# Last stage: shorter turns for eight MLPs, their first squares in the stage in front, earlier experts, a quarter of relu on VectorE

## Chip, cores and metric

The kernel runs on one core of one Trainium2 chip. The metric is the device time of one execution in microseconds (us), as the median of several runs. A profiled execution, recorded by the hardware profiler, gives the span and everything that is said below of single instructions.

## The reference, cut to what matters

The input x has 16 sequences of 256 tokens with 128 features, 4096 tokens in all. Eight sublayers follow each other, each as `x = x + layernorm(f(layernorm(x)))`. The change lies in the seventh sublayer's last part and the eighth sublayer:

```python
# end of L3_attn_ref: attention, then a squared-relu MLP
xa = xa + attn_scale * (y @ o_w)
xa = xa + a_mlp_scale * (square(relu(rms_norm(xa) @ a_fc_w)) @ a_proj_w)   # 128 -> 512 -> 128
# L3_ffn_ref: 8 experts; each expert takes the 64 best of a sequence's 256 tokens
probs = softmax(x @ gate_w)                    # per token over 8 experts
g, m = top_k(probs per expert, 64)
h = gelu(x[m] @ w1[e]) @ w2[e]                 # 128 -> 512 -> 128
out = zeros; out[m] += g * h                   # rounded to bf16
```

Around both stands the outer norm: `x = x + layernorm(xa)`, then `layernorm(x)` is what the experts read, then `x = x + layernorm(out)` is the result.

## The kernel before

All data stay on the chip. The tokens lie in eight groups g = 0 to 7 of 512 tokens (two sequences), each a tile of 128 partitions x 4 x 128 (`xm[g]`, `x[g]`). Work that belongs together is a Python generator; each `yield` ends a step. `Ctx.turns` writes the instruction order by hand: time is counted in turns, an item starts at a given turn, and in each turn every started item gives one step (up to three if it is behind), in the order of the list. Instructions go to their engine's queue in just this order, and each queue is worked through in order. So the start turns and the places of the `yield`s decide what stands in front of what on each engine.

`stage_last` has three kinds of items. `last(g)` is the MLP of one group and what follows it: squares (L1727, GpSimd), their sum (L1730, VectorE), `rsqrt` (L244 and L245, GpSimd), the scaled n (L1735, VectorE), four transposes on TensorE and the copy nT (L1739, ScalarE), four products with `afc` into PSUM (128x512 each, called afc below), each followed by Relu (L1745) and Square (L1746) on ScalarE, sixteen products with `aproj` (called aproj below), the copy ln_y (L1751, ScalarE), the sum with xm (L1753, VectorE), layer norm statistics (L255 and L257 on VectorE, L244 and L245 on GpSimd), the norm (L264, VectorE), the sum into x (L1757, GpSimd), statistics of x, nb = -mean x rs (L1716 and L1717, GpSimd), the normed `exn` on ScalarE (L1720), its transposes and copy xT (L1764), the gate product (128x8), its copy p (L1772), and the softmax into `probs` (L1775 to L1783). `selection(q)` takes the probabilities of two groups, transposes them (L1791), and picks 64 of 256 tokens in eight rounds on VectorE (L1797 and L1799), then the rank of each chosen token by three small products and `slot` (L1818). `pair_of(q, pair)` does two experts for four sequences: one-hot matrices `hot` (L1828, VectorE) and `back` (L1832, GpSimd), the gather as a product into `ps_xin`, transposes of `back` (L1850), products with w1, gelu (L1866), products with w2, and the weighted scatter as a product into `ps_sum`.

Before, `last(g)` starts in the turns 0, 1, 3, 5, 7, 9, 19 and 21, `selection(q)` in 19, 25, 33 and 42, and the first pair of experts in turn 25, the others two turns apart. Groups 6 and 7 thus stand partly among the experts. PSUM has five banks that rotate for nearly all of this (`ps_s`), one for `ps_xin` and two for `ps_sum`.

The stage in front, `l3_gqa` over `attention_stage`, is the attention of the same groups. Its `tail(g)` ends with the sum of the attention output into xm (L1644, GpSimd). In that stage the ScalarE alternates between Exp and Sqrt, and each change is a table load (L1585 for Sqrt, L491 for Exp). Between the two stages the work pool changes, so the first tiles of the last stage wait for the end of what read the old ones, the sum L1644 of group 7 among it.

Of the kernel before, what the change touches and what calls it, by code (L numbers as in the profile page):

```python
# [24 lines left out]
AF = mybir.ActivationFunctionType  # L25
ALU = mybir.AluOpType
AX = mybir.AxisListType
PSUM = bass.MemoryType.PSUM

NB, SEQ, P, D = 16, 256, 128, 128  # L30
NG, NT, GT = 8, 4, 512
# [10 lines left out]
RMS_EPS = float(np.finfo(np.float32).eps)  # L42
# [143 lines left out]
def idle(n):  # L186

    for _ in range(n):
        yield


def bc(ap, axis, n):

    ap = ap.unsqueeze(axis)
    shape = list(ap.shape)
    shape[axis] = n
    return ap.to_broadcast(shape)
# [1408 lines left out]
def l3_gqa(k, xa, w, gain, first):  # L1606

    nc, v = k.nc, k.nc.vector  # L1610

    def head(g, got):
        if g == 0:
            yield
            rot, vs = first
        else:
            rot, vs = yield from l3_rotated(k, xa[g], w)
        yield
        ps = k.transposed_ps(rot, slice(P, 2 * P))
        got["kT"] = k.t([P, GT], "kT", 3)  # L1620
        nc.scalar.copy(got["kT"], ps)
        yield
        got["qT"] = k.t([P, GT], "qT", 2)
        v.tensor_scalar(got["qT"], k.transposed_ps(rot, slice(0, P)), gain, 1.0 / math.sqrt(8.0), ALU.mult, ALU.mult)
        yield
        got["km"] = k.variants(got["kT"], "km")
        yield from idle(6)

        for t in range(NT):
            src = vs[:, t, :].rearrange("p (r d) -> p r d", r=4)  # L1630
            to = k.vm[g % 2][:, t].rearrange("p v (r n) -> p v r n", r=4)
            for u in range(2):
                nc.scalar.copy(to[:, u::2, :, 16 * u : 16 * u + 8], bc(src, 1, 2))
        yield from idle(2)
        got["qm"] = k.variants(got["qT"], "qm")
        yield

    def tail(g, yT):
        yield
        ps = k.tokens_ps(yT, w["o"])  # L1640
        y = k.t([P, NT, D], "y", 2)
        nc.scalar.copy(y, ps)
        yield
        nc.gpsimd.tensor_tensor(xa[g], xa[g], y, ALU.add)  # L1644
        yield

    k.attention_stage(head, 26, 1, tail)


# [52 lines left out]
def stage_last(k, x, xm, w, xn, probs, out):  # L1702
# [4 lines left out]
    nc, v = k.nc, k.nc.vector  # L1707
    ident, ones = k.c["ident"], k.c["ones"]
    ne, cap, nb = 8, 64, 4
    iota = k.c["iota"].rearrange("p (e c) -> p e c", e=2)  # L1710
    slots, sums = {}, {}

    def normed(out, src, mv, rs):

        nb = k.t([P, NT], "ln_nb", 3)
        nc.gpsimd.tensor_scalar(nb, mv[:, :, 0], -1.0, None, ALU.mult)  # L1716
        nc.gpsimd.tensor_tensor(nb, nb, rs, ALU.mult)  # L1717
        yield from idle(2)
        for t in range(NT):
            nc.scalar.activation(  # L1720
                out[:, t, :], src[:, t, :], AF.Identity, bias=nb[:, t : t + 1], scale=rs[:, t : t + 1]
            )

    def last(g):
        xg = xm[g]
        sq = k.t([P, NT, D], "rms_sq", 2)
        nc.gpsimd.tensor_tensor(sq, xg, xg, ALU.mult)  # L1727
        yield
        ss = k.t([P, NT], "rms_ss", 3)
        v.tensor_reduce(ss, sq, AX.X, ALU.add)  # L1730
        rs = k.t([P, NT], "rms_rs", 3)
        k.rsqrt(rs, ss, 1.0 / D, RMS_EPS)
        yield from idle(2)
        n = k.t([P, NT, D], "n", 2)
        v.tensor_tensor(n, xg, bc(rs, 2, D), ALU.mult)  # L1735
        yield
        ps = k.transposed_ps(n)
        nT = k.t([P, GT], "nT", 2)
        nc.scalar.copy(nT, ps)  # L1739
        yield  # L1740
        h = k.t([P, 4, GT], "mlp_h", 4)
        for i in range(4):
            ps = k.ps("s")
            k.mm(ps, w["afc"][:, i * P : (i + 1) * P], nT)
            nc.scalar.activation(h[:, i, :], ps, AF.Relu)  # L1745
            nc.scalar.activation(h[:, i, :], h[:, i, :], AF.Square)  # L1746
            if i % 2:
                yield
        ps = k.tokens_ps(h, w["aproj"].rearrange("p (c n) -> p c n", c=4))
        y = k.t([P, NT, D], "ln_y", 3)  # L1750
        nc.scalar.copy(y, ps)  # L1751
        yield
        v.tensor_tensor(y, y, xg, ALU.add)  # L1753
        mv, rs = k.stats(y)
        yield from idle(2)
        k.normed(y, y, mv, rs)
        nc.gpsimd.tensor_tensor(x[g], x[g], y, ALU.add)  # L1757
        yield
        mv, rs = k.stats(x[g])
        yield from normed(xn[g], x[g], mv, rs)  # L1760
        yield
        ps = k.transposed_ps(xn[g])
        xT = k.t([P, GT], "xT", 2)
        nc.scalar.copy(xT, ps)  # L1764
        yield


        ps = k.ps("s")
        for t in range(NT):
            k.mm(ps[:, t * ne : (t + 1) * ne], xT[:, t * P : (t + 1) * P], w["gate"])  # L1770
        p = k.t([P, NT, ne], "p", 3)
        nc.scalar.copy(p, ps[:, : NT * ne].rearrange("p (t e) -> p t e", t=NT))  # L1772
        yield
        m = k.t([P, NT], "pm", 3)
        v.tensor_reduce(m, p, AX.X, ALU.max)  # L1775
        v.tensor_tensor(p, p, bc(m, 2, ne), ALU.subtract)
        nc.scalar.activation(p, p, AF.Exp)
        yield
        v.tensor_reduce(m, p, AX.X, ALU.add)
        v.reciprocal(m, m)  # L1780
        for b in range(2):
            at, ts = (2 * g + b) * ne, slice(2 * b, 2 * b + 2)
            v.tensor_tensor(probs[:, :, at : at + ne], p[:, ts, :], bc(m[:, ts], 2, ne), ALU.mult)  # L1783
        yield

    def selection(q):

        rows = nb * ne
        ps = k.ps("s")
        for t in range(2):  # L1790
            nc.tensor.transpose(ps[:rows, t * P : (t + 1) * P], probs[:, t, rows * q : rows * (q + 1)], ident)  # L1791
        cur = k.t([rows, SEQ], "top", 2)
        nc.scalar.copy(cur, ps[:rows, :SEQ])
        yield
        for n in range(cap // 8):
            best = k.t([rows, 8], "best", 2)
            v.max(out=best, in_=cur)  # L1797
            nxt = k.t([rows, SEQ], "top", 2)
            v.match_replace(out=nxt, in_to_replace=best, in_values=cur, imm_value=-1.0)  # L1799
            cur = nxt  # L1800
            if n in (2, 5):
                yield
        chosen = k.t([rows, SEQ], "chosen", 1)
        v.tensor_scalar(chosen, cur, 0.0, None, ALU.is_lt)
        yield
        ps = k.ps("s")
        for t in range(2):
            nc.tensor.transpose(ps[:, t * rows : (t + 1) * rows], chosen[:, t * P : (t + 1) * P], ident[:rows, :rows])
        mk = k.t([P, 2, rows], "mk", 2)
        nc.scalar.copy(mk, ps[:, : 2 * rows].rearrange("p (t r) -> p t r", t=2))  # L1810
        yield

        rank = k.ps("s")[:, : 2 * rows].rearrange("p (t r) -> p t r", t=2)
        k.mm(rank[:, 0, :], k.c["before"], mk[:, 0, :])
        k.mm(rank[:, 1, :], ones, mk[:, 0, :], True, False)
        k.mm(rank[:, 1, :], k.c["before"], mk[:, 1, :], False, True)
        slot = slots[q] = k.t([P, 2, rows], "slot", 3)
        v.scalar_tensor_tensor(slot, rank, 1.0, mk, ALU.add, ALU.mult)  # L1818
        v.tensor_scalar(slot, slot, -1.0, None, ALU.add)
        yield  # L1820
# [82 lines left out]

    items = []
    for q in range(4):
        items += [(25 + 8 * q + 2 * pair, pair_of(q, pair)) for pair in range(4)]
    items = items[::-1] + [((19, 25, 33, 42)[q], selection(q)) for q in range(4)]
    items += [((0, 1, 3, 5, 7, 9, 19, 21)[g], last(g)) for g in range(NG)]
    with k.tc.manual_schedule():
        k.turns(items)  # L1910

# [2 lines left out]
def program(ctx: ExitStack, tc: tile.TileContext, xin, dram, at, out):  # L1914
# [92 lines left out]
    with pool("first", "left") as pf:  # L2007
        first = []
        stage("l3m", "left", stage_trunk, l2, rows1["l2b2"], l3, rows3, lm, xm, first, pf, banks=MAMBA_BANKS)
        closed("lm")  # L2010
        with phase("l3g", RING_BANKS):
            l3_gqa(k, xm, l3, l3["gain"], first)
# [4 lines left out]
    en = [pd.tile([P, NT, D], F32, tag=f"exn{g}", name=f"exn{g}") for g in range(NG)]  # L2017
    probs = pd.tile([P, 2, NB * 8], F32, tag="probs", name="probs")
    stage("last", "left", stage_last, xm, last, en, probs, out, banks=LAST_BANKS)
    closed("wd")  # L2020
    closed("we")
# [24 lines left out]
```

## Time and profile before

| what | value |
|---|---|
| median of 3 runs | 2974.41 us (2969.55 to 2975.85) |
| profiled execution | 2974.3 us, its span 2972.5 us |
| mean granted TensorE clock | 0.964 |
| TensorE matmul busy | 2756.0 us, 93% of the span |
| VectorE, ScalarE, GpSimd busy | 1930.3, 1675.4, 1020.9 us |
| last stage | from 2662 us to the end at 2972.5 us |
| TensorE busy from 2660 to 2970 us | 280 of 310 us |

Start times below are us from the start of the span. In the tables by stretch of time the columns are length, then busy time (and instructions) of TensorE matmuls, weight loads, VectorE, ScalarE and GpSimd, then the granted TensorE clock (1.00 is full speed), the DMA share and GB/s. In the chain of waits each row is start, length, engine, tile and line. In a timeline a row is start, length, engine, line, operation, out<-in and count, with the idle time in front and what ended it in brackets. TensorE's fp32 products are recorded as two passes each, so four afc are eight records.

### The profile page before, as it was taken

Reading aid. Unit: us, or ns where it says so; the run is one execution under the profiler, and the core shown is the slowest. Engines: PE = TensorE matmul, PEld = TensorE weight load, DVE = VectorE, ACT = ScalarE, POOL = GpSimd, SP = SyncE. Lnnn points to the kernel's source line nnn. Section 1 sums busy time; section 2 is a strip of 40 time slices with the busy share of each in tenths; the row PEclk is TensorE's granted clock in tenths of the full one; section 3 lists DMA queues with packets and bytes.
Section 4 is the critical chain, followed back from the end, with each engine's and each line's share of the span. In section 5 each row is a group of like instructions: output and inputs, shape, how many; then the busy total and the mean of one; then the engine's idle time right before and its main releaser. Section 6 shows DMA issues by size and latency. Waiting matters only on the chain.

```text
span 2972.5 us, 59427 instructions
## 1 busy us (share of the span) xinstructions
PE 2756.0 (93%) x23673; PEld 1878.9 (63%) x23674; DVE 1930.3 (65%) x5300; ACT 1675.4 (56%) x3528; POOL 1020.9 (34%) x1407
## 2 busy tenths in 40 slices
PE   8889999999998799999978997899999699978998
PEld 4556766777666588888753443566666344436897
DVE  5666465564666889999866774566665577635441
ACT  6745556455565667777735665344443277756543
POOL 3553333333336100000044554323231456544332
PEclk9989999999999899999988999899999799988999
DMA  4000000000001000000020000000000000010000
GB/s 116 12 1 2 1 2 2 1 2 1 1 2 37 1 16 8 9 8 9 12 68 5 1 1 1 1 1 1 1 1 1 1 1 1 1 48 10 2 16 15
DMA packets 29149, 31.29 MB, mean 11 GB/s; under 512 B 7292, under 2 KB 20156, under 8 KB 28732
## 3 DMA queue, kind: packets, MB, share of 16 engines
q1 hardware_dynamic: 28872, 27.49, 3.1%
q8 instruction: 187, 3.06, 0.4%
q14 instruction: 90, 0.74, 0.1%
HBM read 23.29 MB, written 4.19 MB: 9 GB/s over the span
## 4 chain that ended last, share of the span: by engine, by line
PE 51%; ACT 7%; DVE 6%; POOL 2%; issue 2%; POOLq 0%; ACTq 0%; DVEq 0%
PE ps_s L336 32%; PE ps_o L336 7%; PE ps_mm L336 6%; ACT at_e L491 1%; PE ps_s L325 1%; ACT lg L1199 1%; PE ps_xin L336 1%; ACT meT L1206 1%; PE ps_sum L336 1%; ACT mdisp L1106 1%; ACT lg L1079 1%; PE ps_t L1204 1%; DVE at_nm L459 1%; PE ps_s L525 1%; POOL ln_rs L245 1%
## 5 line engine op out<-in xcount | busy, mean ns | idle before, releaser
L459 DVE TENSOR_REDUCE at_nm<-ps_s 128x2 f32<-128x512 f32 (+1 forms) x384 | 238.0, 681 | 125.1 <-PE ps_s L336 125.1
L491 ACT ACTIVATE at_e<-ps_s 128x512 f32<-128x512 f32 x384 | 198.1, 604 | 94.1 <-PE ps_s L336 91.9
L1480 DVE TENSOR_TENSOR scan<-ps_s,lm 128x384 f32<-128x384 f32 x256 | 124.6, 549 | 143.2 <-PE ps_s L336 142.9
L497 POOL TENSOR_SCALAR_AFFINE_SELECT at_e<-at_e 128x1024 f32<-128x1024 f32 (+1 forms) x96 | 135.1, 1408 | 209.5 <-ACT at_e L491 209.1
L245 POOL TENSOR_TENSOR ln_rs<-ln_rs,mhalf 128x4 f32<-128x4 f32 x192 | 196.3, 1022 | 15.2
L1015 POOL TENSOR_TENSOR ln_rs<-ln_mv,mendt 128x4 f32<-128x4 f32 x6 | 1.2, 199 | 521.2 <-DVE ln_mv L1013 521.2
L891 DVE TENSOR_REDUCE l_max<-ps_s 128x3 f32<-128x384 f32 x256 | 124.0, 548 | 61.6 <-PE ps_s L336 61.6
L336 PE MATMUL ps_o<-my,meT 128*128 128x129 f32 x1024 | 144.0, 288 | 20.9 <-ACT mgot L1218 17.1
L336 PEld LDWEIGHTS ps_s<-l_w,mlp_h 128*128 128x128 f32 x1280 | 149.5, 192 | 19.8 <-issue 15.1
L336 PE MATMUL ps_s<-l1f_phi,mxT 128*128 128x256 f32 x512 | 141.8, 401 | 21.5 <-DVE mpart L1080 15.7
L244 POOL TENSOR_SCALAR ln_rs<-ln_mv 128x4 f32<-128x4 f32 x184 | 39.6, 215 | 331.9 <-DVE ln_mv L257 312.6
L336 PEld LDWEIGHTS ps_o<-my,meT 128*128 128x128 f32 x1024 | 127.8, 195 | 39.3 <-ACT mgot L1218 22.3
L336 PE MATMUL ps_s<-km,qT 32*128 32x512 f32 x768 | 139.4, 665 | 14.0 <-POOL km L383 12.7
L336 PE MATMUL ps_s<-l_w,mlp_h 128*128 128x128 f32 x1280 | 150.4, 275 | 1.2 <-ACT mlp_h L824 0.9
L336 PE MATMUL ps_s<-qm,kT 32*128 32x512 f32 x768 | 143.0, 651 | 7.7 <-DVE at_nm L459 7.6
L941 POOL TENSOR_SCALAR_AFFINE_SELECT e<-e 128x512 f32<-128x512 f32 x128 | 78.6, 635 | 172.9 <-ACT e L938 172.9
L336 PE MATMUL ps_o<-at_e,at_vm 128*32 128x128 f32 (+1 forms) x2048 | 123.6, 338 | 15.2 <-ACT at_oT L521 15.2
L336 PE MATMUL ps_mm<-mdisp,mxn 128*128 128x128 f32 x1024 | 125.3, 279 | 5.0 <-DVE mdisp L1118 4.9
L938 ACT ACTIVATE e<-ps_s 128x384 f32<-128x384 f32 x256 | 105.5, 513 | 39.5 <-PE ps_s L336 39.4
L336 PEld LDWEIGHTS ps_mm<-mdisp,mxn 128*128 128x128 f32 x1024 | 121.8, 195 | 7.9 <-DVE mdisp L1118 6.6
L1457 ACT COPY BT<-ps_s 128x512 f32<-128x512 f32 x64 | 37.5, 586 | 154.6 <-PE ps_s L336 154.6
L336 PE MATMUL ps_s<-xT,l_w 128*128 128x512 f32 x256 | 119.7, 597 | 3.8 <-ACT mlp_h L824 2.7
(456 smaller groups left out, 7135.9 us busy)
## 6 DMA issues: line engine op xcount, KB each, us to landing
mw<-in_l1fw SPq DMA_DIRECT2D x16, 256.0 KB, 2.6
moe_w<-in_moe SPq DMA_DIRECT2D x16, 256.0 KB, 5.3
l_w<-in_l SPq DMA_DIRECT2D x10, 256.0 KB, 3.3
x<-in_x SPq DMA_DIRECT2D x8, 256.0 KB, 5.4
xs<-x SPq DMA_DIRECT2D x8, 256.0 KB, 2.1
out<-x SPq DMA_DIRECT2D x8, 256.0 KB, 2.3
slT<-xs SPq DMA_DIRECT2D x6, 256.0 KB, 2.7
l1f_phi<-in_l1f SPq DMA_DIRECT2D x1, 1024.0 KB, 5.0
```

Source lines behind the costliest of these rows:

```text
L244: g.tensor_scalar(out, in_, scale, eps, ALU.mult, ALU.add)
L245: g.tensor_tensor(out, out, self.mhalf[:, :n], ALU.pow)
L325: self.nc.tensor.transpose(out[:n, k * P : (k + 1) * P], src[:, k, cols], self.c["ident"])
L336: self.nc.tensor.matmul(out, lhsT=lhsT, rhs=rhs, start=start, stop=stop, skip_group_check=True)
L459: v_.tensor_reduce(nm[:, t, r, vs], s, AX.X, ALU.max, negate=True)
L491: nc.scalar.activation(e[:, r], s, AF.Exp)
L497: nc.gpsimd.affine_select(at, at, [[0, 4], [0, n], [1, P]], ALU.is_ge, 0.0, base=0, channel_multiplier=-1)
L891: v.tensor_reduce(mx[:, b, :, h, 16], s, AX.X, ALU.max, negate=True)
L938: nc.scalar.activation(e[:, h].rearrange("p j n -> p (j n)"), s[:, : 3 * P], AF.Exp)
L941: nc.gpsimd.affine_select(e[:, :, j, :], e[:, :, j, :], [[0, 4], [1, P]], ALU.is_ge, 0.0, base=0, channel_multiplier=-1)
L1457: nc.scalar.copy(s, ps)
L1480: v.tensor_tensor(m, s[:, : SEQ + P], lm[:, SCAN_HEADS[4 * (t // 2) + 2 * i + hh], :], ALU.mult)
```

## The change

Five edits, all in the last two stages. (1) The sum of squares of group 0 is taken in the stage in front, by four ScalarE Squares with accumulation right after the sum into xm, and its `rsqrt` goes into `kept[0]`; `last(0)` starts with n. (2) `last(g)` has fewer idle turns: three waits of two turns are one each, and the statistics of x use the shared helper `stats_nb` (the same GpSimd instructions), so that a group takes 14 turns. (3) The start turns of `last(g)` become 0, 0, 2, 3, 5, 7, 12, 15, of `selection(q)` 16, 24, 32, 40, and the first experts start in turn 23. (4) Of the four Relus of a group the second runs on VectorE as a maximum with 0. (5) The local helper `normed` goes.

```diff
@@ l3_gqa, tail
         nc.gpsimd.tensor_tensor(xa[g], xa[g], y, ALU.add)
         yield
+        if g == 0:
+
+            ss = k.t([P, NT], "last_ss", 1)
+            sq = k.t([P, D], "last_sq", 1)
+            for t in range(NT):
+                nc.scalar.activation(sq, xa[g][:, t, :], AF.Square, accum_out=ss[:, t : t + 1])
+            yield
+            k.rsqrt(k.kept[0], ss, 1.0 / D, RMS_EPS)
@@ stage_last
     def last(g):
         xg = xm[g]
-        sq = k.t([P, NT, D], "rms_sq", 2)
-        nc.gpsimd.tensor_tensor(sq, xg, xg, ALU.mult)
-        yield
-        ss = k.t([P, NT], "rms_ss", 3)
-        v.tensor_reduce(ss, sq, AX.X, ALU.add)
-        rs = k.t([P, NT], "rms_rs", 3)
-        k.rsqrt(rs, ss, 1.0 / D, RMS_EPS)
-        yield from idle(2)
+        rs = k.kept[0]
+        if g:
+            sq = k.t([P, NT, D], "rms_sq", 2)
+            nc.gpsimd.tensor_tensor(sq, xg, xg, ALU.mult)
+            yield
+            ss = k.t([P, NT], "rms_ss", 3)
+            v.tensor_reduce(ss, sq, AX.X, ALU.add)
+            rs = k.t([P, NT], "rms_rs", 3)
+            k.rsqrt(rs, ss, 1.0 / D, RMS_EPS)
+            yield
...
             k.mm(ps, w["afc"][:, i * P : (i + 1) * P], nT)
-            nc.scalar.activation(h[:, i, :], ps, AF.Relu)
+            if i == 1:
+                v.tensor_scalar(h[:, i, :], ps, 0.0, None, ALU.max)
+            else:
+                nc.scalar.activation(h[:, i, :], ps, AF.Relu)
             nc.scalar.activation(h[:, i, :], h[:, i, :], AF.Square)
...
         mv, rs = k.stats(y)
-        yield from idle(2)
+        yield
         k.normed(y, y, mv, rs)
         nc.gpsimd.tensor_tensor(x[g], x[g], y, ALU.add)
         yield
-        mv, rs = k.stats(x[g])
-        yield from normed(xn[g], x[g], mv, rs)
+        nb, rs = k.stats_nb(x[g])
+        yield
+        k.normed_act(xn[g], x[g], nb, rs)
         yield
...
-        items += [(25 + 8 * q + 2 * pair, pair_of(q, pair)) for pair in range(4)]
-    items = items[::-1] + [((19, 25, 33, 42)[q], selection(q)) for q in range(4)]
-    items += [((0, 1, 3, 5, 7, 9, 19, 21)[g], last(g)) for g in range(NG)]
+        items += [(23 + 8 * q + 2 * pair, pair_of(q, pair)) for pair in range(4)]
+    items = items[::-1] + [((16, 24, 32, 40)[q], selection(q)) for q in range(4)]
+    items += [((0, 0, 2, 3, 5, 7, 12, 15)[g], last(g)) for g in range(NG)]
```

The helpers that the new lines call were there before: `stats_nb` (L266) is `stats` and the two GpSimd operations of nb, and `normed_act` (L279) the four ScalarE Identities.

## The prediction

> **What bounds the kernel now.** I read the last stage by stretches of time first, because the kernel's average (TensorE 93% busy) mixes stages with different limits.
>
> ```profile
> 2660.00:2670.00 10.00, 2.28 (x14) 1.93 (x14) 1.97 (x3) 0.96 (x2) 5.79 (x7) 0.63 0.49 151
> ...
> 2690.00:2700.00 10.00, 9.16 (x49) 6.10 (x48) 7.24 (x28) 6.51 (x13) 7.39 (x11) 1.00 0.01 2
> ...
> 2730.00:2740.00 10.00, 4.96 (x18) 3.23 (x18) 9.56 (x47) 3.89 (x12) 7.53 (x13) 0.54 0.00 0
> ...
> 2770.00:2780.00 10.00, 10.00 (x80) 8.99 (x80) 2.49 (x11) 5.50 (x11) 2.94 (x5) 1.00 0.01 2
> ```
>
> The reader is to see three parts. At 2660 TensorE waits for the first MLP. From 2690 on it is nearly full. Between 2730 and 2740 it is half empty and nearly at half clock (which lasts to 2754.7) while VectorE has 9.56 of 10 us busy: this is the gap between six MLPs and the first experts. From 2770 TensorE is full at full clock (I saw the same in every stretch up to 2957), so there only less work can shorten the end. The change can gain at the start and in the gap: TensorE is idle 13.0 us between 2669.3 and 2760 and loses 11.6 us to half clock in it; with 4.9 us of late start the ceiling is 29.5 us.
>
> The chain of waits shows the start:
>
> ```profile
> 2662.35 1.26 POOL xm L1644
> ...
> 2663.69 1.05 POOL rms_sq L1727
> ...
> 2666.84 1.02 POOL rms_sq L1727
> ...
> 2669.31 1.10 PE ps_s L325 x4
> ```
>
> The square of group 0 stands behind the last sum of the stage in front, and its transposes are then held by the square of group 1. Next, the gap in the timeline:
>
> ```profile
> 2741.43 0.57 ACT L1764 COPY xT<-ps_s 128x512 f32<-128x512 f32 x1
> ...
> 2742.05 1.88 PE L336 MATMUL ps_s<-moe_gate,xT 128*128 128x8 f32 x8 [5.43 <-ACT xT L1764]
> ...
> 2757.69 2.51 PE L336 MATMUL ps_s<-l_aproj,mlp_h 128*128 128x128 f32 x21
> ```
>
> TensorE waits 5.43 us for a copy that waits for a softmax step, itself queued behind selection rounds on VectorE. Group 7's second four afc and the projections of groups 6 and 7 come after the gap, as filler between 2753.7 and 2772.5.
>
> **What the Trainium skill says.** "TensorE: Matmul & The Clock Gate", section "What's actually happening": two clock states, half and full, decided over a free-running window of about 3.4 us. The trace agrees: half clock ends at 2676.2, begins at 2730.8 and ends at 2754.7; these are 16 and 7 steps of 3.41 us. "ScalarE: Activation LUTs", section "What ACT_TABLE_LOAD costs": 1283 ns for a load; the loads before the last at_e of the stage in front show 1.28 us. Section "Table sets: the hidden batching unit" says that cheap functions are in every set, and names relu, copy and identity, not Square; in this trace Square runs between Relu and Identity without a load, so I price no load for it. "VectorE: DVE Perf Modes", section "Why PSUM operands drop a tier": an fp32 operand in PSUM keeps VectorE at its basic rate. The trace agrees: a VectorE tensor_scalar of 128x512 out of PSUM (L1293) takes 0.69 us, where ScalarE's Relu takes 0.58.
>
> **The change part by part.** The sum is made against the profiled execution, 2974.3 us (span 2972.5, the median 2974.41, so no offset).
>
> *Start.* For group 0 the GpSimd square, the VectorE sum and two rsqrt operations leave. n then needs only `kept[0]`, long ready, and the end of the last xm sum at 2663.61, because the pool changes there. n takes 0.68, so the transposes start at 2664.45 instead of 2669.31: -4.9 us. The five to six groups behind follow at the same distance as long as the cycle stays.
>
> *Squares in front.* Four Squares of 128 elements (0.41 each, from exn's 1.65 for four) queue on ScalarE behind the first xm sum, in front of a table load, Sqrt, another load and Exp:
>
> ```profile
> 2459.09 1.27 POOL L1644 TENSOR_TENSOR xm<-xm,y 128x512 f32<-128x512 f32 x1
> 2459.26 0.31 ACT L1585 ACTIVATE ss<-ss 128x128 f32<-128x128 f32 x1
> ...
> 2461.06 1.28 ACT L491 ACT_TABLE_LOAD   x1 [1.49 <-PE ps_s L336]
> ...
> 2462.35 2.07 ACT L491 ACTIVATE at_e<-ps_s 128x512 f32<-128x512 f32 x4
> ```
>
> ScalarE is in order, so Sqrt and Exp wait for a sum that they don't need. New: 2460.4 + 1.75 (Squares) + 1.28 + 0.31 + 1.28 = 2465.05 for the first at_e, 2.7 us after 2462.35. TensorE's next scores need the banks that at_e frees; its eight products at 2461.7 already last 2.44 us by that wait. Bounds: 0, if the stage has slack (TensorE is about 90% busy there), and 3.3, if the wait is doubled through the next table change. I take 2.7. A gain is excluded: nothing leaves there. The rsqrt (1.2 us of GpSimd) lies in a GpSimd idle time of 4.1 us; without that cover it would cost its 1.2. No DMA is issued or moved by any edit.
>
> *A quarter of relu on VectorE.* Per group -0.58 us of ScalarE and +0.69 of VectorE. In the cycle of 8.8 us (four afc pairs from 2686.40, 2695.22, 2704.04) TensorE is 9.16 of 10 us busy: afc 3.44 + aproj 3.74 + transposes 1.2 leave under half a us. Groups 0 to 5 thus stay at 8.8; bounds -0.3 each (ScalarE's chain gets shorter) and +0.3 each (the maximum stands in front of a norm step, L264, that exn waits for, and itself behind n). I take 0. Group 5's projections start with the 4.9 us: aproj5 ends at about 2723 instead of 2727.1, a lead of 4 after one more transposition in front.
>
> *Gap.* Groups 6 and 7 start in turns 12 and 15 instead of 19 and 21, so aproj6 3.74, aproj7 3.74, the second half of an afc 3.44 and a set of transposes 0.6, together 11.5 us, stand in front of the first gather instead of behind it, where TensorE was empty. But VectorE carries the gap: to its selection rounds come relu (0.69), sum and statistics (about 1.9) and norm (1.1) of two groups, and `hot` stands behind group 7's ln_y. Following the queues with the durations of the trace, the lead of 4 shrinks to 1.8: first gather at 2754.6 instead of 2756.4. From the first gather to the first w2 product it was 22.9 us (2756.4 to 2779.3), 10.9 of it filler that is now gone; what remains is bound by the chain hot, gather, copy, w1, gelu, about 18.4 us. First w2 at 2773.0: -6.3. Behind it TensorE is full, and its load there is less: exn transposes and gates of groups 6 and 7 (3.2 us before) are done, one transpose of `chosen` (0.3) is now owed: -2.9. Gap and start together: -9.2 (the start's 4.9 is inside, as it carries through to the gap).
>
> *Sum at full clock:* -9.2 + 2.7 = -6.5, with about -0.4 for the waiting start running fewer windows at half clock: -6.9, 2967.4. The shorter turns and `stats_nb` move the same instructions earlier on their queues; their effect is in the numbers of the gap.
>
> *Clock.* The gap had seven windows at half clock. With more work in it some would stay full. If windows drop all the same, products double: +1.7 for an afc, +0.8 for aproj7, up to +3 for the gather phase, less what waits anyway: +3 to +6.
>
> **Rivals.** *Full gain given back to the clock* (same): the gap stays thin because every filler waits for VectorE; -6.9 plus 3 to 6 gives 2970.5 to 2973.5. For it: at 2730 VectorE is 9.56 of 10 us busy, and gets more. Against it: 11.5 us more TensorE work in some 30 us.
>
> *The gap at half clock throughout* (slower): from aproj5 to the first gather TensorE is never busy enough for a window to turn full, so afc6, afc7, aproj6, aproj7 and transposes, 11 to 12 us at full clock, take twice that, and unlike before they stand in front of the first gather: 2754.6 + 12 = 2766.5. The first w2 moves to 2785, less 2.9 of load, plus 2.7: 2974.3 + 5.7 - 2.9 + 2.7 is about 2980, to 2984 if the gather phase stays cold too. It decides from a first gather later than about 2761. For it: before, seven windows were cold although they held 17.6 us of records in 25 us, much of it slow gate products of 8 columns. Against it: afc and aproj are dense.
>
> *The gap closes better* (faster): the maximum on VectorE and the earlier experts shorten the chain hot to w2 as well, and the idle 13 us fill: half of the ceiling of 29.5, about -15, 2959.
>
> *The squares in front hide* (faster, within my forecast's range): cost 0 instead of 2.7 gives 2964.7.
>
> **How the numbers follow.** About 0.2%, 5.9 us, is what a measurement of this kernel can tell from no change: 2968.5 to 2980.3 counts as the same. My forecast, 2967.4 with its own range 2963 to 2970, has 0.40, of which I count 0.37 as faster, as its middle lies only 1 us inside the bound but the uncertain terms (squares, cycle) lean to less time. Better gap at 2959: 0.15, all faster. Gain given back to the clock: 0.29, same. Half clock throughout: 0.16, of which 0.13 beyond 2980.3. That is faster 0.52, same 0.35, slower 0.13. The range reaches from 2957, the better gap, to 2979, part of the cold gap; about 2 in 10 lie outside.
>
> **What would show each step.** Start: the transposes of group 0 between 2 and 6 us earlier against the end of the last xm sum, and no GpSimd square in front. Squares: the first at_e after the first tail later by 2 to 3 us, and the last xm sum of the stage later by as much (2.7; 0 if hidden). Cycle: afc pairs 8.8 us apart; if more, the maximum on VectorE is late. Gap: aproj of groups 6 and 7 in front of the first ps_xin; first ps_xin 2757 with the 2.7 included; 18 us from there to w2; clock at 1.00 or 0.50 in the stretches between. The forecast is wrong if the gap is cold throughout, if the cycle lengthens by more than 0.3 us a group, or if ScalarE's wait in front doubles.

## The result and the profile after

The changed kernel takes 2971.09 us (median of 22 runs, 2967.01 to 2973.53), the kernel before 2975.64 us in 22 runs taken beside them (2969.55 to 2978.72). The ratio is 0.9983, 95% interval 0.9977 to 0.9990: 4.5 us or 0.17% faster, clear of no change and just inside the 0.2% that the prediction called the same. The profiled execution took 2971.42 us, its span is 2969.7.

The two profiled executions can't be laid over each other from their start: the first sum into xm of the stage in front (L1644 of group 0), ahead of which nothing was changed, starts at 2459.09 us before and at 2461.49 after; over the thirteen profiled kernels, all alike up to there, it starts anywhere from 2457.60 to 2461.80. I therefore measure from that sum, and split there: A is from its start to the end of the last such sum (the end of the stage in front), B from there to the end. Before A = 204.52 and B = 308.89; after A = 206.34 and B = 301.87. So between these two executions the stage in front lost 1.8 us and the last stage gained 7.0, and 5.2 in all stand beside the 4.5 of the medians. A and B are given for every run below. Each is read from one execution of its kernel; the times of the kernels are compared by their medians.

The start of the last stage in the timeline of the changed kernel:

```profile
2666.57 1.26 POOL L1644 TENSOR_TENSOR xm<-xm,y 128x512 f32<-128x512 f32 x1 [6.64 <-ACT y L1642]
...
2667.87 0.69 DVE L1734 TENSOR_TENSOR n<-xm,kept 128x512 f32<-128x512 f32 x1 [4.05 <-POOL xm L1644]
...
2668.61 1.11 PE L325 MATMUL ps_s<-const_ident,n 128*128 128x128 f32 x4 [2.74 <-DVE n L1734]
```

n follows the last sum at once and the transposes 0.78 us behind it, where it was 5.70: 4.92 us less, with no GpSimd square between. The price stands in the stage in front, in the same timeline:

```profile
2461.49 1.27 POOL L1644 TENSOR_TENSOR xm<-xm,y 128x512 f32<-128x512 f32 x1
...
2462.79 0.31 ACT L1651 ACTIVATE last_sq<-xm 128x128 f32<-128x128 f32 x1 [2.44 <-POOL xm L1644]
...
2464.51 1.28 ACT L1585 ACT_TABLE_LOAD   x1
...
2467.43 2.06 ACT L491 ACTIVATE at_e<-ps_s 128x512 f32<-128x512 f32 x4
2468.08 2.07 PE L336 MATMUL ps_s<-km,qT 32*128 32x512 f32 x2 [2.72 <-ACT at_e L491]
```

ScalarE stands idle for 2.44 us in front of a Square that waits for the sum, and the table load for Sqrt stands behind four Squares. The first at_e comes 5.94 us after the start of the sum instead of 3.26, and TensorE waits 2.72 us for it.

The table by stretch of time of the changed kernel (columns as before):

```profile
2660.00:2670.00 10.00, 5.24 (x56) 3.48 (x48) 2.07 (x6) 2.11 (x5) 2.81 (x2) 0.75 0.08 14
...
2690.00:2700.00 10.00, 10.00 (x51) 6.54 (x50) 7.49 (x28) 8.88 (x17) 6.85 (x10) 1.00 0.01 2
...
2730.00:2740.00 10.00, 9.38 (x29) 4.87 (x29) 8.15 (x30) 6.41 (x18) 6.98 (x12) 0.67 0.00 0
...
2760.00:2770.00 10.00, 8.22 (x46) 7.17 (x45) 7.89 (x30) 2.90 (x8) 7.99 (x13) 0.66 0.00 1
2770.00:2780.00 10.00, 10.00 (x77) 9.05 (x77) 7.85 (x28) 8.11 (x16) 4.98 (x8) 1.00 0.01 2
```

TensorE's gap is filled (9.38 of 10 us from 2730, before 4.96), but the clock is at half there for part of the time and again from 2760.5 to 2767.3, where the first gathers run. Summed over the last stage up to its final 12 us, TensorE's idle time went from 19.5 to 12.8 us, and what it loses by half clock (busy time times the missing share of the clock) only from 11.5 to 9.1.

The order of the gap, from the timeline:

```profile
2753.47 3.17 PE L336 MATMUL ps_s<-l_aproj,mlp_h 128*128 128x128 f32 x26 [0.66 <-ACT mlp_h L1748]
2757.77 1.48 PE L325 MATMUL ps_s<-const_ident,exn 128*128 128x128 f32 x4 [1.13 <-ACT exn L283]
2759.53 1.21 PE L336 MATMUL ps_xin<-hot,exn 128*128 128x128 f32 x8 [0.28 <-DVE hot L1831]
...
2768.47 1.16 PE L336 MATMUL ps_xin<-hot,exn 128*128 128x128 f32 x8 [1.16 <-ACT xinT L1859]
...
2779.17 3.71 PE L336 MATMUL ps_s<-moe_w,mlp_h 128*64 128x128 f32 x64
```

The projections of group 7 and the exn transposes of group 6 now stand in front of the first gather (2759.53). The third gather (2768.47) is the last product of this phase that TensorE waits for; from it to the first w2 product (2779.17) TensorE has no gap. Measured from the end of the last sum, the lead over before runs as follows: projections of group 0 end 5.97 us earlier, of group 5 5.18, the first gather 1.05 (91.70 against 92.75), the first w2 product 4.35 (111.34 against 115.69), the end 7.02.

### The profile page after: what moved, and what is told of

Read it like the earlier page. It is cut to its first block, busy times and chain, and to the rows that moved or that the text cites. A ratio compares the mean times of both kernels' runs of the same rounds, so it can differ in the third digit from the quotient of the medians.

```text
span 2969.7 us, 59428 instructions
## 1 busy us (share of the span) xinstructions
PE 2755.9 (93%) x23674; PEld 1878.1 (63%) x23674; DVE 1939.3 (65%) x5307; ACT 1671.4 (56%) x3526; POOL 1022.9 (34%) x1406
## 4 chain that ended last, share of the span: by engine, by line
PE 50%; ACT 7%; DVE 6%; POOL 2%; issue 2%; DMA 0%; POOLq 0%; SPq 0%; ACTq 0%; DVEq 0%
PE ps_s L336 32%; PE ps_o L336 7%; PE ps_mm L336 6%; ACT at_e L491 1%; PE ps_s L325 1%; ACT lg L1199 1%; PE ps_xin L336 1%; ACT meT L1206 1%; PE ps_sum L336 1%; ACT mdisp L1106 1%; ACT lg L1079 1%; PE ps_t L1204 1%; DVE at_nm L459 1%; POOL ln_rs L245 1%; PE ps_s L525 1%
## 5 line engine op out<-in xcount | busy, mean ns | idle before, releaser
L336 PEld LDWEIGHTS <-b_ident 128*128 128x128 bf16 x656 | 51.8, 99 | 113.0 <-issue 102.1
```

Of the source, the lines that this page charges most:

```text
L336: self.nc.tensor.matmul(out, lhsT=lhsT, rhs=rhs, start=start, stop=stop, skip_group_check=True)
```

## The experiments

All times, with A and B of the profiled execution:

| kernel | median us | ratio to before, interval | A | B |
|---|---|---|---|---|
| changed | 2971.09 | 0.9983, 0.9977 to 0.9990 | 206.34 | 301.87 |
| e1_no_front_squares | 2975.61 | 0.9997, 0.9989 to 1.0005 | 206.47 | 306.21 |
| b1_before_front_squares | 2973.20 | 0.9995, 0.9987 to 1.0003 | 206.37 | 304.57 |
| e2_squares_later | 2966.89 | 0.9971, 0.9959 to 0.9983 | 202.57 | 302.43 |
| g1_idle_squares_before | 2972.07 | 0.9988, 0.9980 to 0.9996 | 202.30 | 308.05 |
| e3_all_relu_scalar | 2967.87 | 0.9974, 0.9964 to 0.9984 | 206.23 | 300.16 |
| e4_old_starts | 2977.76 | 1.0010, 1.0003 to 1.0016 | 206.36 | 309.84 |
| f2_filler | 2970.63 | 0.9982, 0.9975 to 0.9988 | 206.36 | 302.14 |
| h22_experts_turn_22 | 2970.90 | 0.9981, 0.9974 to 0.9987 | 206.36 | 301.63 |
| c1_later_and_scalar | 2964.31 | 0.9964, 0.9952 to 0.9977 | 202.29 | 300.85 |
| c2_later_relu_six | 2965.60 | 0.9970, 0.9960 to 0.9981 | 202.29 | 303.15 |
| c3_squares_three_turns | 2969.27 | 0.9978, 0.9969 to 0.9987 | 204.43 | 301.37 |

My theory after the result was: the start's 4.9 us are real, ScalarE's wait in front takes 1.8 of them, and half-clock windows in the gather phase (from the first gather to the first w2 product) take 2 to 3. The rivals were that the gap is bound whatever the start is, and that the gather phase is bound by its chain of engines and not by the clock.

**The first edit undone.** `rs` of group 0 comes from GpSimd again:

```diff
@@ l3_gqa, tail
-        if g == 0:
-
-            ss = k.t([P, NT], "last_ss", 1)
...
-            k.rsqrt(k.kept[0], ss, 1.0 / D, RMS_EPS)
@@ stage_last, last
-        rs = k.kept[0]
-        if g:
-            sq = k.t([P, NT, D], "rms_sq", 2)
+        sq = k.t([P, NT, D], "rms_sq", 2)
...
```

> The changed kernel without its first edit: group 0 squares on GpSimd in the last stage again. Theory (the start's 4.9 us carry to the gap, the squares in front cost about 1.8 of them at the end of the stage in front): the last xm sum about 1.8 us earlier, the transposes of group 0 5.7 us after that sum's end instead of 0.8, and the whole 3 us slower than the changed kernel, about 2974. Rival (the gap is bound by VectorE's selection rounds whatever the start is): the first gather does not move with the start, and the time is 2969 to 2971.

It is 4.5 us slower than the changed kernel and can't be told from before: without the first edit, nothing of the gain is left in the medians. In the traces B is 306.21, so that the other edits alone gain 2.7 us in the last stage and the first edit 4.3 more. The start missed its expectation: the transposes of group 0 come 4.16 us after the last sum, not 5.7, and 3.4 us later than in the changed kernel, while the projections of group 0 end 6.6 us later (20.10 against 13.46).

A did not shrink as expected either. The stage in front then has before's instructions, and yet 206.47 against 204.52. Up to group 5's y copy (L1642) the two agree within 0.05 us (169.40 and 169.35 after the first sum). Then the clock falls to half 179.6 us after the first sum in both, and comes back after one window of 3.4 us before (2638.7 to 2642.1), but after two in this run (2641.2 to 2648.0). A further window follows in both. First the kernel before, then this run; the granted clock is the third column from the right:

```profile
2644.00:2648.00 4.00, 4.00 (x54) 1.68 (x50) 0.49 (x2) 2.91 (x7) 1.38 (x2) 1.00 0.02 4
2644.00:2648.00 4.00, 4.00 (x28) 1.12 (x20) 0.62 (x3) 2.06 (x4) 0.55 (x1) 0.50 0.00 0
```

So the same instructions took 2.0 us more or less in this stage. What the first edit costs there is 1.8 us measured against the kernel before and -0.1 against this run; which of the two is the usual case is not known. That led to the grid experiment below.

**The first edit alone.** The same lines put into the kernel before.

> The kernel before with the first edit alone. Theory (the first edit costs 1.8 us by the end of the stage in front and gives 4.9 us at the first transposes, of which the gap, bound by selection rounds queued on VectorE, passes on about 4): 2.5 us faster than before, 2973.2. Rival (the whole difference of the changed kernel is the first edit): 4.5 us faster, 2971.2. Rival (the gap swallows the lead): 1.8 us slower than before, 2977.5.

B 304.57, 4.3 us less than before; A 1.9 more. The sum, -2.5, is what the theory gave; the medians differ by 2.3, but the interval includes no change. Both runs agree that the first edit gives 4.3 us in the last stage. The first gather comes 4.34 us earlier here (88.41 us after the last sum against 92.75), so the gap of the kernel before does not swallow the lead.

**The Squares one turn later.**

```diff
         if g == 0:
-
+            yield from idle(1)
             ss = k.t([P, NT], "last_ss", 1)
```

> The changed kernel with one idle turn in front of the four Squares, so that on ScalarE they stand behind the next Sqrt, its two table loads and four Exp instead of in front of them. Theory (ScalarE in order: Sqrt and Exp waited for an xm sum that they do not need): first at_e of that step 2.5 us earlier, the last xm sum 1.5 to 1.8 us earlier, about 2969.3. Rival (the stage absorbs it, and the difference seen between the two profiles came from elsewhere): the last xm sum does not move, 2971.

In its timeline Sqrt, the load and Exp go ahead, and the Squares follow:

```profile
2460.40 1.27 POOL L1644 TENSOR_TENSOR xm<-xm,y 128x512 f32<-128x512 f32 x1
...
2462.38 1.28 ACT L491 ACT_TABLE_LOAD   x1 [1.49 <-PE ps_s L336]
...
2463.67 2.06 ACT L491 ACTIVATE at_e<-ps_s 128x512 f32<-128x512 f32 x4
...
2465.60 0.33 ACT L1651 ACTIVATE last_sq<-xm 128x128 f32<-128x128 f32 x1
```

The first at_e is back at 3.27 us after the sum. A falls by 3.8 us to 202.57, more than the 2.7 of ScalarE's wait, and the kernel is 4.2 us faster than the changed one. This price of the early place is the firmest reading of A: the six profiled kernels with the Squares where the change has them lie at 206.23 to 206.37, the four with the Squares one turn later at 202.29 to 202.57. One more thing is odd: with more work than before, A is 2.0 us below before's 204.52.

**Work without benefit.** To take this apart, the kernel before got four Squares at this later place, and nothing reads them:

```diff
@@ kernel before, l3_gqa, tail
+        if g == 0:
+            yield
+            ss = k.t([P, NT], "last_ss", 1)
+            sq = k.t([P, D], "last_sq", 1)
+            for t in range(NT):
+                nc.scalar.activation(sq, xa[g][:, t, :], AF.Square, accum_out=ss[:, t : t + 1])
```

> The kernel before with four Squares added on ScalarE in the stage in front, one idle turn behind the first xm sum; nothing reads their result, so this is work and no benefit. Theory (TensorE's half-clock windows lie on a fixed grid to which the kernel is locked; a delay of about 1 us moves the thin end of the stage to other places of the grid, where no window falls to half): at_e chain after the first tail 0.95 us later, but the end of the last xm sum 202.6 us after the start of the first one instead of 204.5, and the whole about 2 us faster than before. Rival (the gain of 2 us at the stage's end comes from something else in the changed kernel): 0.95 us slower than before.

Added work makes the kernel 3.4 us faster (interval 1.2 to 6.0 us from the ratio). The next y copy of the stage (L1642) comes 36.99 us after the one of group 0 instead of 36.05, a delay of 0.94; but the last comes after 205.27 instead of 207.50. The stretches near the stage's end, first of the kernel before:

```profile
2640.00:2644.00 4.00, 4.00 (x36) 1.42 (x32) 0.36 (x1) 1.48 (x4) 0.59 (x1) 0.74 0.00 0
2652.00:2656.00 4.00, 4.00 (x34) 2.08 (x36) 0.84 (x3) 0.58 (x1) 1.66 (x2) 0.57 0.00 0
```

and of the one with the unread Squares:

```profile
2640.00:2644.00 4.00, 4.00 (x44) 1.58 (x44) 0.85 (x3) 2.06 (x4) 1.32 (x2) 1.00 0.02 4
2652.00:2656.00 4.00, 3.24 (x59) 2.04 (x56) 0.85 (x3) 1.13 (x3) 1.28 (x1) 1.00 0.01 4
```

The clock (third column from the right) stays full where it fell before. The changes of the clock lie on a grid of 3.41 us, and in all thirteen profiled kernels this grid lies alike to the work: the fall at the end of the stage in front comes 203.43 to 203.48 us after the start of the first sum, or once, with the later Squares, one step earlier (200.02). So a delay moves the work of the stage against the grid, and with it which steps of the grid are at half clock. The place is not all that decides: in the kernel before and in the first run above the same instructions at the same place had one window and two. Of the 3.4 us, 2.2 lie in A and 0.8 in B.

**The Squares three turns later**, with all Relus on ScalarE (below), tries the same from the other side:

> As the combination of later Squares and all Relus on ScalarE, with three idle turns instead of one in front of the Squares, where they stand behind the next four Exp. Theory (the place of the stage's thin end on the clock's grid counts as much as the delay itself): the delay after the first tail is another one, below 1.7 us; if it is under 0.3 us the two half-clock windows of before come back at the end of the stage, and the whole is about 2 us slower than with one idle turn although less is delayed. Rival (only the delay counts): 0 to 0.9 us faster.

The delay at the next y copy is 1.52 us instead of 0.94, and one half-clock window (2655.0 to 2658.4) appears; A is 204.43 against 202.29, 2.1 more for 0.6 of delay. The whole is 5.0 us slower than with one turn, of which A and B show 2.7. That more counts than the delay alone is borne out; the case that I had named (a delay under 0.3 us, and both windows of before) did not arise.

**All Relus on ScalarE.**

```diff
-            if i == 1:
-                v.tensor_scalar(h[:, i, :], ps, 0.0, None, ALU.max)
-            else:
-                nc.scalar.activation(h[:, i, :], ps, AF.Relu)
+            nc.scalar.activation(h[:, i, :], ps, AF.Relu)
```

> The changed kernel with all four Relus of a group on ScalarE. Theory (the cycle of a group is bound by TensorE, and in the gap VectorE is the fuller engine): the six groups keep their distance, the projections of group 5 end within 0.5 us of the changed kernel, and the gap gets 0.7 to 1.4 us shorter, about 2970. Rival (Relu and Square in one line on ScalarE set the cycle): 0.3 us per group slower, 2973.

3.2 us faster by the medians, 1.7 in B. The guess was right in its direction: group 5 ends 0.8 us later instead of within 0.5 (59.15 us after the last sum against 58.33, so the Relu on VectorE does save 0.14 per group in the cycle), but the first gather comes 1.2 earlier and the first w2 1.7. No window falls to half in the gather phase:

```profile
2750.00:2760.00 10.00, 7.09 (x50) 5.44 (x48) 5.74 (x22) 3.74 (x9) 6.49 (x10) 1.00 0.00 1
2760.00:2770.00 10.00, 8.56 (x55) 6.92 (x54) 9.47 (x39) 7.00 (x15) 5.64 (x11) 1.00 0.01 2
```

Yet from the first gather to the first w2 it still takes 19.1 us (19.6 in the changed kernel). So 1.2 of the 1.7 us are there at the first gather, and 0.6 come in the gather phase, now at full clock.

**Relu on VectorE in six groups only** (`if i == 1 and g < 6`), with the Squares one turn later:

> The changed kernel with the Squares one turn later, and the Relu on VectorE for groups 0 to 5 only. Theory (with all Relus on ScalarE group 5 ended 0.8 us later, so the Relu on VectorE helps the full cycle and costs in the gap, in groups 6 and 7): as the combination with all Relus on ScalarE, and up to 0.8 us faster. Rival (what the Relu on VectorE costs is spread over all groups, or the 0.8 us are lost in the gap): the same as or slower than that combination.

Against the combination of the Squares one turn later with all Relus on ScalarE (last experiment below), group 5 ends 0.8 us earlier, as hoped, but three windows at half clock (2756.8 to 2767.0) stand in the gather phase of this run, which takes 21.2 us instead of 19.1, and B is 2.3 us longer. The profiled execution, 2968.28 us, is one of the two longest of seven (the other five lie at 2964.15 to 2965.62), so these windows need not be typical; the medians differ by 1.3. The theory's gain is not there. Whether the Relus themselves or only the half-clock windows cost it stays open.

**The start turns of before** for groups 6 and 7, the selections and the experts, with all other edits:

```diff
-        items += [(23 + 8 * q + 2 * pair, pair_of(q, pair)) for pair in range(4)]
-    items = items[::-1] + [((16, 24, 32, 40)[q], selection(q)) for q in range(4)]
-    items += [((0, 0, 2, 3, 5, 7, 12, 15)[g], last(g)) for g in range(NG)]
+        items += [(25 + 8 * q + 2 * pair, pair_of(q, pair)) for pair in range(4)]
+    items = items[::-1] + [((19, 25, 33, 42)[q], selection(q)) for q in range(4)]
+    items += [((0, 0, 2, 3, 5, 7, 19, 21)[g], last(g)) for g in range(NG)]
```

> The changed kernel with the start turns of before for groups 6 and 7 (19 and 21), the selections (19, 25, 33, 42) and the experts (25); the first squares in front, the shorter turns and the Relu on VectorE stay. Theory (the start's gain carries only as far as the gap lets it; moving the two groups forward is worth the 2.7 us that the last stage still gained without the first edit): about 2.5 us slower than the changed kernel, 2973.6. Rival (the moved starts are worth nothing, the gain comes from the first edit alone): 2971.

6.7 us slower than the changed kernel and 2.3 slower than before: more than expected. In the gap TensorE waits for group 6's n, which VectorE has queued behind selection rounds, and half clock lasts from 2725.9 to 2749.8, seven windows as before:

```profile
2743.88 1.08 PE L325 MATMUL ps_s<-const_ident,n 128*128 128x128 f32 x4 [6.21 <-DVE n L1734]
```

So these moved starts are worth 8.0 us of B (6.7 by the medians) beside the other edits. The other edits with these old starts cost 5.3 us of B against the first edit alone (309.84 against 304.57; 4.6 by the medians). Which of them does it (the shorter turns, the earlier starts of groups 1 to 5, the Relu on VectorE) was not tried; they pay only together with the moved starts.

**A filler against half clock.** Two unread afc products in front of group 6's exn transposes:

```diff
+        if g == 6:
+            fill = k.ps("s")
+            for _ in range(2):
+                k.mm(fill, w["afc"][:, :P], nT)
         ps = k.transposed_ps(xn[g])
```

> The changed kernel with two more afc products of group 6, whose result is not read, on TensorE in front of the transposes of group 6's exn, in an idle time of 1.1 us. Theory (the two half-clock windows of the gather phase, 2760.9 to 2767.7, cost about 3 us on the way to the first w2): if the filler keeps the window full, the gather phase runs at clock 1.00, the delay of about 0.7 is more than paid back, 2.3 us less, about 2968.8. Rival (the gather phase is bound by the chain hot, back, put, xinT on the other engines): 0.7 us more, 2971.8. If the clock still falls to half, 1.4 us more.

The half clock of the gathers moves from 2760.5 and two windows to one window at 2767.6. The timeline shows the gathers, with a wait for a copy in the middle:

```profile
2759.85 1.16 PE L336 MATMUL ps_xin<-hot,exn 128*128 128x128 f32 x8 [0.29 <-DVE hot L1835]
...
2767.38 1.86 PE L336 MATMUL ps_xin<-hot,exn 128*128 128x128 f32 x8 [1.16 <-ACT xinT L1863]
...
2779.74 3.71 PE L336 MATMUL ps_s<-moe_w,mlp_h 128*64 128x128 f32 x64
```

The first gather is where it was (91.69 us after the last sum), and so, within 0.3 us, is the first w2 (111.58 against 111.34). Halving the half-clock time in this phase brought nothing as a whole, but the two parts of the phase moved. Up to the third gather, where TensorE waits for back and xinT, it takes 7.53 us instead of 8.94, now at full clock. It is 7.53 too in five other runs with at most one window there, among them two with 2.85 us of half clock, so this part is bound by the chain hot, back, put, xinT as long as the clock is not at half for two windows. From the third gather to the first w2 TensorE has no gap, and the part takes 12.36 us instead of 10.70, with the half-clock window now in it (11.53 with all Relus on ScalarE and no window; why it is shorter in the changed kernel stays open). So the rival holds in the size: the two windows of the changed kernel cost about 0.6 us (19.64 against 19.06 at full clock), not 3. Its reason is shown for the first part alone; behind the third gather no gap is left to fill.

**Experts from turn 22** (one digit of the start turns):

> The changed kernel with the first experts in turn 22 instead of 23: on VectorE the first hot stands in front of group 7's sum ln_y instead of behind it, on TensorE the first gather in front of group 6's exn transposes. Theory (hot is ready to run at 2753.6 and waits in line for group 7's projections until 2759.1): first gather about 2.5 us earlier, first w2 about 2 us earlier, 2969. Rival (from the first gather to the first w2 put, xinT and the half clock set the time): first w2 within 0.5 us, 2971; if the later norms of groups 6 and 7 delay the second selection, slower, 2974.

The first gather comes 3.1 us earlier (88.62) and the first w2 1.9, as the theory said, but the end only 0.2. Group 7's gate product (1.06 us) now stands behind the first w2, and ScalarE loads three tables there instead of one, since an Exp of group 7's softmax (L1780) falls between two Gelus (L1869), as its timeline shows:

```profile
2765.86 1.28 ACT L1869 ACT_TABLE_LOAD   x1
...
2768.26 1.28 ACT L1780 ACT_TABLE_LOAD   x1
...
2772.29 1.28 ACT L1869 ACT_TABLE_LOAD   x1
```

How these divide the lost 1.7 us was not tried.

**Both faster edits together** (Squares one turn later, all Relus on ScalarE):

> The changed kernel with the Squares one turn later and all Relus on ScalarE, both edits that were faster alone. Theory (they act in different stages and add): last xm sum 202.6 us after the first one as in the run with the later Squares, 300.2 us from there to the end as in the run with all Relus on ScalarE; 10 to 11 us faster than before, about 2965. Rival (the shift of the grid between the stages undoes part of one): within 1 us of the run with the later Squares, 2967.

2964.31 us, ratio 0.9964 (0.9952 to 0.9977), A and B together 10.3 us less than before. Alone the two edits bring 3.2 and 1.8 us of A and B beyond the changed kernel, together 5.1: they add. It is the fastest kernel of the study, 6.8 us below the changed one; its gap is at half clock only from 2724.4 to 2734.6, as the clock column shows:

```profile
2720.00:2730.00 10.00, 9.09 (x41) 5.66 (x41) 7.47 (x31) 5.20 (x15) 5.25 (x8) 0.72 0.00 0
2730.00:2740.00 10.00, 9.76 (x55) 7.54 (x53) 9.35 (x37) 6.88 (x15) 2.63 (x6) 0.77 0.01 2
2740.00:2750.00 10.00, 9.34 (x57) 6.82 (x55) 5.28 (x30) 5.74 (x13) 4.09 (x7) 1.00 0.00 0
2750.00:2760.00 10.00, 6.35 (x40) 4.36 (x38) 7.07 (x29) 4.32 (x11) 6.21 (x9) 1.00 0.00 1
2760.00:2770.00 10.00, 9.32 (x62) 8.07 (x63) 9.45 (x36) 7.63 (x17) 4.57 (x10) 1.00 0.01 2
```

What is left there is idle time from 2750 to 2760 (6.35 of 10 us busy), in front of and between the first gathers. The kernel was run five times.

## Why the prediction was right in direction and too large in size

Forecast 2967.4, that is -6.9; measured -4.5 (-5.2 in the trace). The range held it, the likeliest case's own range (up to 2970) did not.

- *Start, -4.9.* Right to 0.1 us: -4.92. With the first edit alone, 4.3 of it reach the end.
- *Squares in front, +2.7.* Right as a wait (+2.68 at the first at_e), wrong as a cost of the stage. It was +4.6 at the next y copy, since two windows (2467.0 to 2473.8) fell to half clock, above my bound of 3.3; then the stage's end gave 2.7 back, since the two half-clock windows that it had before were gone. The net of 1.8 lies inside the bounds by luck: two effects meet, neither of which I had, and against the run without the first edit, which has one window more there, the net is -0.1. I had priced the clock for the last stage only. (The sum itself is 2465.02, not 2465.05, and it uses 1.75 us for the Squares where four of 0.41 make 1.64; they took 1.72.)
- *A quarter of Relu, 0.* In the cycle it is -0.14 per group, inside the bounds (the starts that I gave to the afc, from 2686.40 on, are those of aproj; the 8.8 us are the same). From before to the changed kernel the cycle became 0.16 longer by all edits together: the lead at the end of group 0's projections, 5.97, was 5.18 at the end of group 5's, better than my 4. In the gap the Relu costs: with all Relus on ScalarE, B is 1.7 us shorter, 0.6 of it in the gather phase, which then has no half clock. My sum had the Relus of groups 6 and 7 in VectorE's line but took them to be paid within the lead.
- *Gap, -9.2 with the start, and -0.4 for clock.* Measured -7.0. Two terms are mis-sized. From group 5's projections to the first gather I had the lead shrink by 2.2 us (4 to 1.8); it shrank by 4.1 (5.18 to 1.05). In this gap group 6's first two afc products took 3.72 us at half clock, where others take 1.88, which my sum at full clock did not hold; whether they alone cost the 1.9 was not tried. From the first gather to the first w2 I had 18.4 us, bound by its chain of engines; it took 19.64, of which 19.06 stand at full clock and 0.6 are half clock, and the chain binds only the part up to the third gather. After the first w2 it is -2.7 instead of -2.9.
- *Clock.* The rival "full gain given back to the clock" gave 2970.5 to 2973.5, and the time fell there, but not for its reason: half clock cost 2.4 us less than before in the last stage, not more. The cold gap throughout did not come: four windows instead of seven.

So the steps that were read from single waits held to a tenth; what failed was the size of the gap and of the gather phase behind it, which before had been covered by other work, and the clock outside the last stage.

## What to carry to other kernels

An instruction that is put early on an engine in program order takes its own wait with it: look at what stands behind it, and move it behind what need not wait (here one turn was worth 4 us). A small delay far ahead can change which windows run at half clock (0.94 us here took away two), and even the same instructions had one window or two. So a difference of a few microseconds is only understood after the clock of both traces has been compared stage by stage, unchanged stages too, and one trace of each kernel is little. Where filler is taken out of a stretch, measure what it covered, and see for each part of it whether TensorE waits there or is full; do not take it from the sum of its parts.

## What was not expected of the hardware

- Useless work made the kernel faster: with 0.94 us of delay two half-clock windows were gone from the stage in front, and the time was 3.4 us less (g1). "TensorE: Matmul & The Clock Gate" of the Trainium skill, section "What's actually happening", calls the window free-running and the phase variable from run to run. The grid of 3.41 us is there in every trace, but its phase to the work was the same within 0.05 us in all thirteen profiles, each of another kernel. What ties the two together no run shows.
- An activation with accumulation shows a second record of 0.19 us (ACTIVATION_READ_ACCUMULATOR), so four Squares of 128 elements take 1.7 us from 2462.79 to the table load at 2464.51.
